# Adding expert outputs to the result in HBM: full tiles by scatters that add, one load instead of two ahead of the branch

## Chip, cores and metric

One core of one Trainium2 chip. The metric is the device time of one execution in microseconds; the time before is 964.39 us, the median of three runs (959.2 to 976.06).

## What is computed

One transformer block over 4096 tokens of width 256: a linear attention with 16 heads, then a mixture of experts with 8 experts, of which each token uses its two best. The change lies in the last step of the second half:

```python
h = _layernorm(x) * (1 + cb) + sb
gate_probs = softmax(h @ Wg + bg)              # 8 experts
_, top_idx = top_k(gate_probs, 2)
selected = gate_probs * one_hot(top_idx).sum(-2)
selected = selected / (selected.sum(-1, keepdims=True) + 1e-08)
e = gelu(einsum('bsf,efh->bseh', h, W1) + b1)  # hidden width 1024
expert_out = einsum('bseh,ehf->bsef', e, W2) + b2
x = x + gb * einsum('bsef,bse->bsf', expert_out, selected)
```

A token therefore receives two expert outputs, and each is added to its row of the result.

## The kernel before

The first half (attention) leaves the rows of x in SBUF and stores them to the result tensor `out` in HBM. Routing then computes the two experts of every token. Each token's normalised row is written twice into `routed`, a table in HBM with one region per expert, by indirect DMAs that GpSimd issues, 128 rows each (`send`). A row carries its gate weights and its token number; places of the table that no token fills carry a number outside of `out`.

The second half works through **blocks**. A block is 256 or 128 consecutive rows of one expert's region, that is two tiles or one tile of 128 rows. There are 5 early blocks of two tiles (they take only full 256-row blocks of the first 12 of the 32 token tiles), 23 further blocks of two tiles, 8 single blocks that always run, and two groups of single blocks, `once` (4) and `twice` (3), each behind a branch on `left`, a count that routing computes. In the profiled execution `once` runs and `twice` does not, so 40 blocks with 68 tiles run. After the early blocks come seven two-tile blocks, then eight times two two-tile blocks and a single one (`order_of`, lines 1231 to 1234).

For each block, `load` (line 1027) puts five DMAs on SP's queue: `w1` (1 MB), `b1`, the block's rows `xg`, `w2` (1 MB) and `b2`. `prepare` transposes the rows on TensorE, `hidden` (line 1083) makes the first matrix product and the GELU, `project` (line 1101) the second product, and VectorE scales it to tiles `y0` and `y1` of 128 x 256. `run` (line 1241) orders this: at each block it issues the loads of this block and the two that follow, does `hidden` of this block, `prepare` of the next, then `project` and `add_to_out` of the block before. Pools bound how far things run ahead: 3 buffers for `w1`, 4 for `w2`, 4 for `xg` and for each of `y0` and `y1`.

`add_to_out` (line 1122) adds a block's tiles to `out`, all of it on GpSimd's queue: for each tile a gather of its 128 rows of `out` into an SBUF tile `acc` (in profiles `hT<-out_dram,who`, since `acc` lies in an old `hT` buffer), then for each tile a GpSimd addition and a scatter back (`out_dram<-hT,who`). Rows outside of `out` are skipped. Within a block, tiles are declared independent, since a token occurs once per expert; between blocks every gather waits until the scatters of the block before have landed.

Engines issue in the order in which the program's steps are written, up to the last early block (a wrapper, line 28, adds the order; its line 36 is what profiles show for those instructions). After it only GpSimd keeps this order, and a scheduler orders the other engines. Around the early blocks, a table of steps (line 1222) puts the rest of routing between blocks: after block 1's product, the last route's first 16 sends; after block 2's, its last 8 sends and the table of the later blocks; after blocks 2 and 3, the stores of the remaining chunks of `out`.

The main blocks end at the branch (lines 1270 to 1284). Before it, `run(order_of[EARLY:], once[:2])` names two blocks of `once` as following, so that two blocks of `once` are loaded ahead of the branch and the other two inside it.

Of the kernel before, what the change touches and what calls it, by code (L numbers as in the profile page):

```python
# [15 lines left out]
ALU = mybir.AluOpType  # L16
# [8 lines left out]
BT = BLK // P  # L25
# [23 lines left out]
def adaln_block_kernel(  # L49
# [18 lines left out]
    on = SimpleNamespace(pe=nc.tensor, dve=dve, act=nc.scalar, pool=nc.gpsimd, sp=nc.sync)  # L68
# [18 lines left out]
    EARLY = 5  # L87
# [53 lines left out]
    token = const.tile([P, NCH, TPC], I32, tag="token", name="token")  # L141
# [51 lines left out]
    with tc.tile_pool(name="attn", bufs=1) as attn, tc.tile_pool(  # L193
# [24 lines left out]
        at = KB * P + E * HB  # L218
# [256 lines left out]
        with tc.tile_pool(name="ps_c", bufs=1, space=bass.MemoryType.PSUM) as ps_c:  # L475
# [83 lines left out]
            for s in range(NT + LAG):  # L559
# [6 lines left out]
                if s >= LAG:  # L566
                    add_context(s - LAG)
                    after_context(s - LAG)
                    i, rest = divmod(order[s - LAG], 3)
# [121 lines left out]
    def parked(i: int):  # L691
        return hT[i].rearrange("p kb (z d) -> p (kb z) d", d=D)
# [326 lines left out]
    w2_v = w2.rearrange("e (hb p) f -> e p hb f", p=P)  # L1019
    IN_RANGE = "the table holds rows and experts that exist"  # L1020

    accs = [parked(0)[:, BT * z : BT * (z + 1), :] for z in range(2)]

    def tiles_of(b: int):
        return BT if b < EARLY + PAIRED else 1
# [1 line left out]
    def load(b: int):  # L1027
        nt = tiles_of(b)
        first = nc.values_load(
            where[0:1, 0, b : b + 1], engines=[ENG.SP], min_val=0, max_val=E * N - nt * P,  # L1030
            skip_runtime_bounds_check_because=IN_RANGE,
        )
        e = nc.values_load(
            where[0:1, 1, b : b + 1], engines=[ENG.SP], min_val=0, max_val=E - 1,
            skip_runtime_bounds_check_because=IN_RANGE,
        )
        w1_sb = w1_pool.tile([P, KB, H], FP, tag="w1", name="w1_sb")
        on.sp.dma_start(w1_sb, w1_v[ds(e, 1)].squeeze(0))
        b1_sb = xpool.tile([P, HB], FP, tag="b1", name="b1_sb")
        on.sp.dma_start(b1_sb, b1_d[ds(e, 1)].squeeze(0))  # L1040
        xg = xpool.tile([P, BT, ROW], FP, tag="xg", name="xg")
        ins = on.sp.dma_start(
            xg[:, :nt, :], routed[ds(first, nt * P), :].rearrange("(j p) w -> p j w", p=P)
        )
        if b < EARLY:
            apart(ins, early_loads, later_sends)
        w2_sb = w2_pool.tile([P, HB, D], FP, tag="w2", name="w2_sb")
        on.sp.dma_start(w2_sb, w2_v[ds(e, 1)].squeeze(0))
        b2_sb = xpool.tile([P, D], FP, tag="b2", name="b2_sb")
        on.sp.dma_start(b2_sb, b2_d[ds(e, 1)].squeeze(0).partition_broadcast(P))  # L1050
        return xg, w1_sb, b1_sb, w2_sb, b2_sb

    def prepare(b: int, xg):

        nt = tiles_of(b)
        xT = bpool.tile([P, KB, BLK], FP, tag="xT", name="xT")
        for kb in range(KB):
            pt = ps_b.tile([P, BLK], FP, tag="b", name="ptb")
            for j in range(nt):
                on.pe.transpose(  # L1060
                    pt[:, j * P : (j + 1) * P], xg[:, j, kb * P : (kb + 1) * P], ident
                )
            on.act.activation(  # L1063
                xT[:, kb, : nt * P], pt[:, : nt * P], AF.Identity,
                bias=mod_sb[:, 2, kb : kb + 1], scale=mod_sb[:, 3, kb : kb + 1],
            )
        return xT

    def weights_of(b: int, xg):

        nt = tiles_of(b)
        who = npool.tile([P, BT], I32, tag="who", name="who")
        on.dve.tensor_copy(who[:, :nt], xg[:, :nt, D + E].bitcast(I32))  # L1073
        g = bpool.tile([P, BT, E], FP, tag="g", name="g")
        on.dve.tensor_tensor(
            g[:, :nt, :], xg[:, :nt, D : D + E],
            mine[:, b : b + 1, :].to_broadcast([P, nt, E]), ALU.mult,
        )
        gs = npool.tile([P, BT], FP, tag="gs", name="gs")
        on.dve.tensor_reduce(gs[:, :nt], g[:, :nt, :], AX.X, ALU.add)  # L1080
        return who, gs

    def hidden(b: int, xT, b1_sb, w1_sb):
        rows = tiles_of(b) * P
        gl = bpool.tile([P, HB, BLK], FP, tag="gl", name="gl")
        for hb in range(HB):
            ph = ps_a.tile([P, BLK], FP, tag="a", name="ph")
            for kb in range(KB):
                on.pe.matmul(  # L1089
                    ph[:, :rows],  # L1090
                    w1_sb[:, kb, hb * P : (hb + 1) * P],
                    xT[:, kb, :rows],
                    start=(kb == 0),
                    stop=(kb == KB - 1),
                )
            on.act.activation(  # L1096
                gl[:, hb, :rows], ph[:, :rows], AF.Gelu_apprx_tanh, bias=b1_sb[:, hb : hb + 1]
            )
        return gl

    def project(b: int, gl, w2_sb, b2_sb, who, gs):

        ys = []
        for j in range(tiles_of(b)):
            py = ps_b.tile([P, D], FP, tag="b", name="py")
            for hb in range(HB):
                on.pe.matmul(  # L1107
                    py,
                    gl[:, hb, j * P : (j + 1) * P],
                    w2_sb[:, hb, :],  # L1110
                    start=(hb == 0),
                    stop=(hb == HB - 1),
                )
            y = xpool.tile([P, D], FP, tag=f"y{j}", name="y")
            on.dve.scalar_tensor_tensor(y, py, gs[:, j : j + 1], gb_bc, ALU.mult, ALU.mult)  # L1115
            on.dve.scalar_tensor_tensor(y, b2_sb, gs[:, j : j + 1], y, ALU.mult, ALU.add)
            ys.append(y)
        return ys

    n_added = 0  # L1120

    def add_to_out(b: int, ys, who):
        nonlocal n_added
        acc = accs[n_added % len(accs)]
        n_added += 1
        rows = FIRST * TPC * P if b < EARLY else N
        done = []
        for j in range(len(ys)):
            ins = on.pool.indirect_dma_start(
                acc[:, j, :], None, out[0, :rows], IndirectOffsetOnAxis(ap=who[:, j : j + 1], axis=0),  # L1130
                bounds_check=rows - 1, oob_is_err=False,
            )
            done.append((j, ins))
        for j, y in enumerate(ys):
            on.pool.tensor_tensor(acc[:, j, :], acc[:, j, :], y, ALU.add)
            ins = on.pool.indirect_dma_start(
                out[0, :rows], IndirectOffsetOnAxis(ap=who[:, j : j + 1], axis=0), acc[:, j, :], None,
                bounds_check=rows - 1, oob_is_err=False,
            )
            for i, other in done:  # L1140
                if i != j:
                    tc.declare_no_dep(
                        ins.ins, other.ins, reason="a token is at most once among an expert's rows"
                    )
            done.append((j, ins))


    on.pe, on.dve, on.act, on.pool, on.sp = (
# [82 lines left out]
    order_of = list(range(EARLY + PAIRED - 2 * FIXED))  # L1231
# [3 lines left out]
    once = [EARLY + PAIRED + FIXED + j for j in range(ONCE)]  # L1235
# [29 lines left out]
    def flush():  # L1265
        nonlocal pending
        add_to_out(pending[0], project(*pending), pending[-2])
        pending = None

    done = set()  # L1270
# [3 lines left out]
        left[0:1, 0:1], min_val=UNITS, max_val=UNITS + ONCE + TWICE,  # L1274
        skip_runtime_bounds_check_because=IN_RANGE,
    )
    run(order_of[EARLY:], once[:2])
    flush()
    with tc.If(n_left > UNITS):  # L1279
        run(once, [])  # L1280
# [35 lines left out]
```

## Time and profile before

| | |
|---|---|
| median of 3 runs | 964.39 us |
| the profiled execution | 958.09 us |
| its span in the profile | 956.4 us |
| TensorE busy | 864.0 us, 90% of the span |
| GpSimd busy | 402.9 us, 42% |
| gathers of `out` rows, `hT<-out_dram,who` | 68, 1047 ns of GpSimd each, 4.9 us median to landing |
| scatters, `out_dram<-hT,who` | 68, 1018 ns of GpSimd each, 4.9 us median to landing |
| GpSimd additions of two 128 x 256 tiles | 68, 737 ns each |
| sends, `routed<-row,dest_i` | 64, 1048 ns of GpSimd each, 2.5 us median to landing |
| HBM read and written | 122.02 MB and 57.71 MB |

PE is TensorE, DVE VectorE, ACT ScalarE, POOL GpSimd and SP the engine whose queue issues the loads. In a timeline each line gives start, duration, engine, source line, operation, output from input, and in brackets how long the engine had been idle before and what ended that. In the table of windows each line gives the window, its length, and the busy time of each engine with its number of instructions.

### The profile page before, as it was taken

The page shows a single profiled execution, that of the slowest core. Times are in us where ns is not written, and L with a number is a line of the kernel's source. Part 1 is how long each engine was busy: PE and PEld are TensorE (multiplying, and loading weights), DVE is VectorE, ACT ScalarE, POOL GpSimd, SP SyncE. Part 2 cuts the span into 40 slices and gives each one's busy share as a digit, 9 for nine tenths or more (in the row PEclk, how much of TensorE's full clock was granted, in tenths as well). Part 3 has the DMA queues.
Part 4 walks back from the last instruction along what each step waited for, and adds up shares of the span by engine and source line. Part 5 has one row for each costly group of instructions (what it writes and reads, how often), then busy time and mean ns, then how long its engine had stood idle before and what let it go on. Part 6 is the DMA issues. An engine that isn't in the chain of part 4 may idle for free. (4 is left out here: it accounts for less than half of the span.)

```text
span 956.4 us, 12974 instructions
## 1 busy us (share of the span) xinstructions
PE 864.0 (90%) x4578; PEld 648.8 (68%) x4578; DVE 386.1 (40%) x943; ACT 347.9 (36%) x638; POOL 402.9 (42%) x377
## 2 busy tenths in 40 slices
PE   7979999999999795699779999999999999999760
PEld 4544444555545574578668888898888888888650
DVE  4454553988888747767312111111111112111110
ACT  4314442344344334455322332333333333342410
POOL 2000000588989507465744343443433433334532
PEclk9979999999999997789979999999999999999985
DMA  9999930132000013595488666677777777777510
GB/s 334 351 344 351 351 102 22 59 115 70 1 1 2 1 45 111 196 363 211 142 314 291 227 194 220 218 250 237 255 232 238 254 240 226 247 239 236 162 46 14
DMA packets 122952, 179.57 MB, mean 188 GB/s; under 512 B 12957, under 2 KB 101571, under 8 KB 122885
## 3 DMA queue, kind: packets, MB, share of 16 engines
q1 hardware_dynamic: 113040, 152.78, 49.3%
q0 software_dynamic: 9840, 25.93, 7.8%
q8 instruction: 37, 0.61, 0.3%
q14 instruction: 31, 0.25, 0.1%
q10 hardware_dynamic: 4, 0.00, 0.0%
HBM read 122.02 MB, written 57.71 MB: 188 GB/s over the span
## 5 line engine op out<-in xcount | busy, mean ns | idle before, releaser
L1096 ACT ACTIVATE gl<-ph,b_sb 128x256 f32<-128x256 f32 (+1 forms) x280 | 122.5, 438 | 273.8 <-PE ph L1089 267.4
L1107 PE MATMUL py<-w_sb,gl 128*128 128x256 f32 x960 | 214.3, 381 | 0.0
L1089 PE MATMUL ph<-xT,w_sb 128*128 128x256 f32 (+1 forms) x1120 | 207.5, 343 | 0.6 <-ACT xT L1063 0.6
L1089 PEld LDWEIGHTS ph<-xT,w_sb 128*128 128x128 f32 x1120 | 184.5, 191 | 20.4 <-ACT xT L1063 0.8
L1107 PEld LDWEIGHTS py<-w_sb,gl 128*128 128x128 f32 x960 | 180.9, 191 | 23.5
L1115 DVE SCALAR_TENSOR_TENSOR y<-py,gs,gb_bc 128x256 f32<-128x256 f32 x60 | 28.9, 482 | 269.8 <-PE py L1107 261.5
L36 POOL DMA_INDIRECT hT<-out_dram,who x68 | 71.2, 1047 | 152.6 <-DMA out_dram<-hT,who 134.6
L277 PE MATMUL pq<-wq,hT 128*128 128x512 f32 x256 | 118.3, 604 | 1.2 <-DVE qs L36 1.2
L277 PE MATMUL pk<-wk,hT 128*128 128x512 f32 x256 | 115.7, 604 | 0.3 <-ACT hT L178 0.3
L36 POOL TENSOR_TENSOR hT<-hT,y 128x256 f32<-128x256 f32 x68 | 50.1, 737 | 110.6 <-DMA hT<-out_dram,who 104.3
L36 POOL DMA_INDIRECT routed<-row,dest_i x64 | 67.1, 1048 | 61.3 <-DVE st L36 19.3
L277 PEld LDWEIGHTS pk<-wk,hT 128*128 128x128 f32 x256 | 48.1, 194 | 59.8 <-issue 54.7
L277 PEld LDWEIGHTS pq<-wq,hT 128*128 128x128 f32 x256 | 46.0, 189 | 49.5 <-issue 45.9
L36 POOL DMA_INDIRECT out_dram<-hT,who x68 | 69.2, 1018 | 19.0 <-POOL hT L36 18.2
L36 POOL TENSOR_TENSOR qs<-qs,qsum 128x1024 f32<-128x1024 f32 x30 | 58.1, 1938 | 15.6 <-DVE qsum L36 15.6
L36 DVE TENSOR_TENSOR qs<-qs,pk 128x1024 f32<-128x1024 f32 x31 | 37.8, 1221 | 62.0 <-ACT ka L438 43.8
L1073 DVE COPY who<-xg 128x2 int32<-128x2 int32 (+1 forms) x35 | 6.1, 173 | 109.4 <-DMA xg<-routed 99.4
L483 POOL MEMSET qs<- 128x8 f32 x8 | 0.9, 117 | 112.0 <-PE pt L175 80.8
L36 ACT ACTIVATE qs<-qs 128x1024 f32<-128x1024 f32 x32 | 33.8, 1055 | 38.1 <-DVE qs L36 38.1
L438 ACT ACTIVATE ka<-pk 128x1024 f32<-128x1024 f32 x24 | 24.6, 1024 | 57.2 <-PE pk L277 57.2
L36 DVE TENSOR_REDUCE qmax<-pq 128x16 f32<-128x1024 f32 x32 | 38.6, 1206 | 13.9 <-PE pq L277 13.8
L36 POOL TENSOR_TENSOR ka<-ka,nk_bc 128x1024 f32<-128x1024 f32 x18 | 42.4, 2358 | 0.0
(253 smaller groups left out, 954.8 us busy)
## 6 DMA issues: line engine op xcount, KB each, us to landing
w_sb<-in_L_ffn_W_dram SPq DMA_DIRECT2D x80, 1024.0 KB, 5.6
routed<-pad SPq DMA_DIRECT2D x32, 1088.0 KB, 13.1
x<-in_L_attn_x_dram SPq DMA_DIRECT2D x16, 512.0 KB, 6.8
xg<-routed SPq DMA_DIRECT2D x28, 272.0 KB, 5.3
b_sb<-b_d SPq DMA_DIRECT2D x40, 128.0 KB, 5.2
out_dram<-x SPq DMA_DIRECT2D x8, 512.0 KB, 5.3
xg<-routed SPq DMA_DIRECT2D x12, 136.0 KB, 5.3
ka<-in_L_wmod_dram SPq DMA_DIRECT2D x3, 512.0 KB
```

The source lines that it names most:

```text
L36: ins = getattr(self.engine, name)(*args, **kwargs)
L277: nc.tensor.matmul(pw[:, half * 512 : (half + 1) * 512], hT[i][:, kb, t * P : (t + 1) * P], w[:, kb, half * 512 : (half + 1) * 512], start ...
L438: nc.scalar.activation(k_tile(n), pk, AF.Identity)
L483: nc.gpsimd.memset(qs[:, :, (h + 1) * HW - 1 : (h + 1) * HW], 1.0)
L1073: on.dve.tensor_copy(who[:, :nt], xg[:, :nt, D + E].bitcast(I32))
L1089: on.pe.matmul(ph[:, :rows], w1_sb[:, kb, hb * P : (hb + 1) * P], xT[:, kb, :rows], start=(kb == 0), stop=(kb == KB - 1),)
L1096: on.act.activation(gl[:, hb, :rows], ph[:, :rows], AF.Gelu_apprx_tanh, bias=b1_sb[:, hb : hb + 1])
L1107: on.pe.matmul(py, gl[:, hb, j * P : (j + 1) * P], w2_sb[:, hb, :], start=(hb == 0), stop=(hb == HB - 1),)
L1115: on.dve.scalar_tensor_tensor(y, py, gs[:, j : j + 1], gb_bc, ALU.mult, ALU.mult)
```

## The change

Tiles that can't hold skipped rows are added by the DMA itself: an indirect scatter from `y` to `out` with addition as its operation, with no gather, no GpSimd addition and no `acc`. These are both tiles of the early blocks and the first tile of the 23 other two-tile blocks, 33 of the 68 that run. The last tile of every other block may be partial and is treated as before, in the order gather, scatter that adds for the full tile, addition, scatter. Each of the two `acc` buffers holds one tile instead of two. The blocks of `once` that are named as following, and so loaded ahead of the branch, are one instead of two.

```diff
@@ add_to_out
-        for j in range(len(ys)):
+        partial = None if b < EARLY else len(ys) - 1
...
+        if partial is not None:
+            acc = accs[n_added % len(accs)]
+            n_added += 1
             ins = on.pool.indirect_dma_start(
-                acc[:, j, :], None, out[0, :rows], IndirectOffsetOnAxis(ap=who[:, j : j + 1], axis=0),
-                bounds_check=rows - 1, oob_is_err=False,
+                acc, None, dest, index(partial), bounds_check=rows - 1, oob_is_err=False
             )
...
         for j, y in enumerate(ys):
-            on.pool.tensor_tensor(acc[:, j, :], acc[:, j, :], y, ALU.add)
+            if j != partial:
+                ins = on.pool.indirect_dma_start(
+                    dest, index(j), y, None, bounds_check=rows - 1, compute_op=ALU.add
+                )
+                apart_from_others(ins)
+        if partial is not None:
+            on.pool.tensor_tensor(acc, acc, ys[partial], ALU.add)
+            done.pop(0)
             ins = on.pool.indirect_dma_start(
-                out[0, :rows], IndirectOffsetOnAxis(ap=who[:, j : j + 1], axis=0), acc[:, j, :], None,
-                bounds_check=rows - 1, oob_is_err=False,
+                dest, index(partial), acc, None, bounds_check=rows - 1, oob_is_err=False
             )
...
-    run(order_of[EARLY:], once[:2])
+    run(order_of[EARLY:], once[:1])
```

`apart_from_others` declares the DMAs of one block's tiles independent, as the loop before did.

More of the change, by code (lines that the diff above doesn't have):

```diff
@@ L1020, in adaln_block_kernel @@
     IN_RANGE = "the table holds rows and experts that exist"
-    accs = [parked(0)[:, BT * z : BT * (z + 1), :] for z in range(2)]
+    accs = [parked(0)[:, z, :] for z in range(2)]
     def tiles_of(b: int):
@@ L1123, in add_to_out, with index, apart_from_others @@
         nonlocal n_added
-        acc = accs[n_added % len(accs)]
-        n_added += 1
         rows = FIRST * TPC * P if b < EARLY else N
+        dest = out[0, :rows]
+        partial = None if b < EARLY else len(ys) - 1
         done = []
-        for j in range(len(ys)):
+        def index(j):
+            return IndirectOffsetOnAxis(ap=who[:, j : j + 1], axis=0)
+        def apart_from_others(ins):
+            for other in done:
+                tc.declare_no_dep(
+                    ins.ins, other.ins, reason="a token is at most once among an expert's rows"
+                )
+            done.append(ins)
+        if partial is not None:
+            acc = accs[n_added % len(accs)]
+            n_added += 1
             ins = on.pool.indirect_dma_start(
-                acc[:, j, :], None, out[0, :rows], IndirectOffsetOnAxis(ap=who[:, j : j + 1], axis=0),
-                bounds_check=rows - 1, oob_is_err=False,
+                acc, None, dest, index(partial), bounds_check=rows - 1, oob_is_err=False
             )
-            done.append((j, ins))
+            done.append(ins)
         for j, y in enumerate(ys):
-            on.pool.tensor_tensor(acc[:, j, :], acc[:, j, :], y, ALU.add)
+            if j != partial:
+                ins = on.pool.indirect_dma_start(
+                    dest, index(j), y, None, bounds_check=rows - 1, compute_op=ALU.add
+                )
+                apart_from_others(ins)
+        if partial is not None:
+            on.pool.tensor_tensor(acc, acc, ys[partial], ALU.add)
+            done.pop(0)
             ins = on.pool.indirect_dma_start(
-                out[0, :rows], IndirectOffsetOnAxis(ap=who[:, j : j + 1], axis=0), acc[:, j, :], None,
-                bounds_check=rows - 1, oob_is_err=False,
-            )
[L1140 to L1145, printed above, removed]
+                dest, index(partial), acc, None, bounds_check=rows - 1, oob_is_err=False
+            )
+            apart_from_others(ins)
     on.pe, on.dve, on.act, on.pool, on.sp = (
```

## Prediction

> **What bounds the kernel now.** I read the chain of waits first. It names GpSimd's round trips to HBM:
>
> ```profile
> DMA 31%; POOL 8%; issue 8%; POOLq 1%
> DMA hT<-out_dram,who 19%; DMA out_dram<-hT,who 13%; POOL hT L36 5%; POOL out_dram L36 3%; POOLq L36 1%; POOLq L1273 0%; POOLq L1279 0%
> ```
>
> A chain that ends last needn't have set the pace, so the table of windows comes next:
>
> ```profile
> 560.00:600.00 40.00, 40.00 (x191) 35.20 (x191) 6.95 (x21) 12.71 (x27) 14.67 (x16) 1.00 0.68 218
> 910.00:957.00 47.00, 13.96 (x77) 12.22 (x75) 2.91 (x6) 2.95 (x8) 13.93 (x15) 0.68 0.06 19
> ```
>
> From 520 to 880 PE is busy 40.00 of every 40 us at clock 1.00. There the additions are hidden; taking them away earns nothing. Time can be won where PE is idle after routing: at 473 to 484, and from 901. The timeline of the first place, PE, then SP, then POOL:
>
> ```profile
> 465.72 7.07 PE L36 MATMUL ph<-xT,w_sb 128*128 128x256 f32 x32
> 484.26 1.09 PE L36 MATMUL ptb<-ident,xg 128*128 128x128 f32 x4 [11.48 <-DMA xg<-routed]
> ```
> ```profile
> 457.64 0.40 SPq L36 DMA_DIRECT2D w_sb<-in_L_ffn_W_dram  x1
> ...
> 481.00 0.39 SPq L36 DMA_DIRECT2D xg<-routed  x1
> ```
> ```profile
> 460.76 0.97 POOL L36 DMA_INDIRECT routed<-row,dest_i  x1 [0.31 <-issue]
> 462.04 1.06 POOL L36 DMA_INDIRECT hT<-out_dram,who  x1 [0.30 <-issue]
> ...
> 468.20 1.02 POOL L36 DMA_INDIRECT out_dram<-hT,who  x1 [0.28 <-POOL hT L36]
> 469.52 0.97 POOL L36 DMA_INDIRECT routed<-row,dest_i  x1 [0.30 <-issue]
> ```
>
> PE waits 11.48 us for the rows of the first later block; SP can't load them before the last send has landed; and the last 8 sends stand on POOL behind block 0's two gathers, additions and scatters (462.04 to 469.52). The second place, the last four blocks (`once`), PE and then SP:
>
> ```profile
> 897.88 3.73 PE L1089 MATMUL ph<-xT,w_sb 128*128 128x128 f32 x32
> 907.87 0.69 PE L1060 MATMUL ptb<-ident,xg 128*128 128x128 f32 x2 [6.25 <-DMA xg<-routed]
> 908.35 5.13 PE L1107 MATMUL py<-w_sb,gl 128*128 128x256 f32 x16
> ```
> ```profile
> 883.77 0.33 SPq L1050 DMA_DIRECT2D b_sb<-b_d  x1
> 901.65 0.38 SPq L1038 DMA_DIRECT2D w_sb<-in_L_ffn_W_dram  x1
> 902.27 0.33 SPq L1040 DMA_DIRECT2D b_sb<-b_d  x1
> 903.13 0.33 SPq L1042 DMA_DIRECT2D xg<-routed  x1
> ```
>
> SP holds the fourth block's `w1` from 884 until PE has finished the third block's hidden product (897.88 + 3.73 = 901.61). Its `xg` is queued behind; PE idles 6.25 us, and the product after it runs slower (5.13 us; the same 16 matmuls took 3.62 at 894.43). Last, POOL's end:
>
> ```profile
> 942.70 0.72 POOL L36 TENSOR_TENSOR hT<-hT,y 128x256 f32<-128x256 f32 x1 [1.65 <-DMA hT<-out_dram,who]
> 943.70 0.99 POOL L36 DMA_INDIRECT out_dram<-hT,who  x1 [0.28 <-POOL hT L36]
> ```
>
> The last `y` is ready at 925.08 (DVE 924.59 + 0.49), its addition starts 17.6 us later. POOL trails all the way: a `y` of 537.6 is added at 559.05, one of 887.3 at 915.44. So the end is POOL's backlog.
>
> **What the Trainium skill says.** Page "DMA: Bandwidth & Descriptors", section "SWDGE vs HWDGE vs iDMA": an accumulating DMA can only be issued by GpSimd; the new scatters stay on this queue. "Rules for kernel authors": the accumulate reads its destination and writes it later, so blocks still have to wait for each other; no duration is given and the trace has none. "Anatomy of one DMA": about 2.0 us plus bytes/436e3, an estimate of 2.3 us for 131072 bytes. The quiet tail agrees for plain ones (gather issue 940.02 to addition 942.70: 2.68), the loaded stage doesn't (median 4.9). "Issuing engines are not separate DMA queues": all share 16 engines, which is why loads stretch these DMAs.
>
> **Part 1, early blocks: -6.2 us.** The built order of instructions shows block 0's first scatter-add ahead of the 16 sends, its second between the 16 and the 8. The first needs `y0`, ready at 435.15, while POOL idles until 440.41: hidden, and only a `y0` later than 440.41 would push the sends back, one for one. Between 461.73 (460.76 + 0.97) and the eighth-last send then stands one issue: 461.73 + 0.30 + 1.02 + 0.30 = 463.35 instead of 469.52, so 6.17 us. I price the issue like a plain scatter (1.02); at 2 us, 5.2 remain. Last send, SP's `xg` and behind it `w2`, three stores and the next block's loads all move with it; PE idles 5.3 instead of 11.5. Next late is block 6's `xg` (VectorE gets it at 498.1, PE needs it at 500.45), and it stands on the same queue and moves too.
>
> **Part 2, the load: -8.1 us.** The early load of `once`'s second block goes behind SP's branch. SP gets there after the first block's `b2` at 859.11 and that `w1` has a wait for PE until 864.91 anyway, so 5.4 us cover a branch that now takes at most 2.2 (873.46 to 875.61). What counts is the buffers: with two `w1` tiles taken outside the branch only one of three rotates inside, hence the wait for the third block. In the changed program's waits, the fourth `w1` waits for the second block's hidden product: 894.2 (890.54 + 3.84 less overlap) instead of 901.61. `xg` follows at 895.8, lands at 900.5 with the 4.74 us of before (903.13 to 907.87), before PE's 901.6. PE gains 6.25, plus 1.5 (5.13 - 3.62) and 0.3 for the cold transposes.
>
> **Part 3, POOL's backlog: -13.9 us.** Per later two-tile block one gather (1.04 + 0.31), one addition (0.74) and one scatter (1.02) go, one scatter-add (1.02 + 0.31) comes. In series after the gather lands, 0.72 + 0.28 + 1.02 + 0.04 + 0.74 + 0.28 + 1.01 = 4.1 becomes 2.0. POOL's cycle of 14.1 (551.25 to 565.38) would be about 12 against PE's 14.25 (ptb 500.45 to 514.70); two pairs and a single, about 32 against 35.7. Over 7 pairs and 8 such triples that is some 45 us of room for a 22 us backlog. The early blocks, with no gather, should already clear most of it. POOL then waits for `y`. A scatter-add waiting for `y0` holds back only the addition and scatter of `y1`, which comes later still; the two smaller `acc` cost nothing, as a gather waits for the scatters before it anyway. With zero backlog, the tail in the old time, moved by part 2: `y` at 887.3, 899.2, 905.9, 913.3, 916.8; each single costs a landing of 2.4, a gather to addition of 2.7 and 1.0, some 6.1, more under loads; the last scatter goes at about 921.5, 4.7 after its `y` against 18.6 (943.70 - 925.08).
>
> The unknown is X, a scatter-add's issue to landing. From below 2.5 (the sends), from above 9.8 (a gather and a scatter in series, 4.9 each); below 2.5 I exclude, it also reads. I take 6. Inside these ends it is hidden: it starts with `y0`, 3.5 us before `y1`, and the other scatter lands 6 us after `y1`. VectorE's next write of `y0` waits for it, four blocks on. Moving about 33 x 128 KB less to SBUF in the PE-bound stage earns nothing.
>
> **Sum.** 6.2 + 8.1 + 13.9 = 28.2. From the last scatter to the end stay 12.7 us (956.4 - 943.70). Span 928.2; with the 1.7 around it 929.9. The median shown is 1.0066 of the profiled execution, so 936.
>
> **Rivals.** (a) *The backlog stays.* The gather of 551.25 comes 0.5 us after a `w2` load (550.74), the scatters beside a `w1` load (557.65): POOL may be held on the loads' beat, and fall back onto it. Against: the saved 2 us put the next gather at 562.5, between two loads. Then part 2 doesn't reach the end, since POOL needs no earlier `y`; part 1 and some 3 us of the last pairs remain: 947 span, 955. (b) *The load doesn't come earlier*, SP being held at the branch: 28.2 - 8.1 leaves 936.3, 944. (c) *Slower: the scatter-add is slow.* POOL's pair takes 1.36 + X; two and a single (10.5, 766.33 to 776.82) exceed PE's 35.7 from X = 11.2. Once four `y` buffers are full, PE stalls. At X = 14: first gather at 522, 7 x 15.4 + 8 x 41.2 + 3 x 6.4 gives 979 for the last, +3.7 and +12.7 an end of 995, or 1003. For it: a read and a write per row on DMA engines that are 0.64 to 0.78 busy; against: plain round trips sum to 9.8.
>
> **Chances.** All three parts 0.66, 923 to 944 alone (X and the tail's landings). (a) 0.13, (b) 0.09, (c) 0.09, else 0.03. The range 923 to 955 leaves out (c) and half the rest. 2% is about what a measurement here tells from no change: faster means below 945.1; this holds most of the first case and half of (b), so 0.70; (a) and rests 0.19; slower 0.11.
>
> **What would show it.** The eighth-last send starts near 463 and PE's wait there is near 5 us; no PE wait ahead of the fourth `once` block; POOL's additions waiting for `y` on VectorE from 600 on, and the last scatter within 6 us of the last `y`. Wrong, if scatter-adds land after more than 11 us, or if PE shows gaps between 520 and 880.

## The result, and the profile after

The changed kernel takes 957.3 us (median of 20 runs, 952.34 to 962.63), the kernel before 968.93 (20 runs beside it, 959.20 to 976.06). The ratio is 0.9889, 95% interval 0.9866 to 0.9913: 1.1% faster, where 2.9% was forecast. The profiled execution took 959.75 us with a span of 958.0. The profile of before (958.09) was quicker than any of these 20 runs of before, so the two profiles can't be subtracted; each stage has to be read by itself.

In the text blocks are counted from 0: block 5 is the first after the five early ones. The expectations on record call it "the fifth block", and what they call the third early block is block 3.

The chain of waits of the changed kernel, where the one of before had DMA and POOL at its head and no PE:

```profile
PE 81%; DVE 6%; another core or an unknown queue 4%; POOL 2%; DMA 2%; issue 2%; ACT 2%; POOLq 0%; ACTq 0%; DVEq 0%
```

POOL's round trips are gone from it. The 4% of "an unknown queue", some 38 us on a kernel that runs on one core, wasn't in the chain of before.

**From block 5 on, the forecast came true but for the tail.** The table of windows (the window, its length, the busy time of PE, PE's weight loads, DVE, ACT and POOL with their instructions, the clock, DMA share and GB/s):

```profile
560.00:600.00 40.00, 40.00 (x193) 35.23 (x192) 5.70 (x17) 13.62 (x29) 12.07 (x12) 1.00 0.69 215
910.00:957.00 47.00, 27.14 (x182) 24.89 (x180) 5.32 (x20) 12.56 (x35) 13.98 (x15) 0.85 0.21 69
```

PE is full as before, and the last 47 us hold 27 us of PE work where they held 14. The timeline of the fourth `once` block, PE and then SP:

```profile
919.84 3.73 PE L1089 MATMUL ph<-xT,w_sb 128*128 128x128 f32 x32
923.41 0.38 PE L1060 MATMUL ptb<-ident,xg 128*128 128x128 f32 x2
923.63 3.62 PE L1107 MATMUL py<-w_sb,gl 128*128 128x256 f32 x16
```
```profile
916.36 0.38 SPq L1038 DMA_DIRECT2D w_sb<-in_L_ffn_W_dram  x1
...
917.84 0.33 SPq L1042 DMA_DIRECT2D xg<-routed  x1
```

No bracket stands ahead of the transposes (6.25 us before): `w1` was issued at 916.36, ahead of the third block's product (919.84), and the next product takes 3.62 instead of 5.13. POOL's end:

```profile
944.17 1.05 POOL L36 DMA_INDIRECT hT<-out_dram,who  x1 [1.59 <-DMA out_dram<-hT,who]
947.04 0.72 POOL L36 TENSOR_TENSOR hT<-hT,y 128x256 f32<-128x256 f32 x1 [1.82 <-DMA hT<-out_dram,who]
948.03 1.00 POOL L36 DMA_INDIRECT out_dram<-hT,who  x1 [0.28 <-POOL hT L36]
```

The last `y` is ready at 938.83 (DVE 938.35 + 0.48), the last scatter goes 9.2 us later instead of 18.6, and the end comes 10.0 after it instead of 12.7.

**Ahead of block 5 something else happened.** PE, then ACT, around block 3's hidden product:

```profile
468.50 0.47 PE L36 MATMUL ph<-xT,w_sb 128*128 128x256 f32 x1 [0.37 <-issue]
483.30 2.07 PE L36 MATMUL ph<-xT,w_sb 128*128 128x256 f32 x4 [14.33 <-issue]
```
```profile
454.80 0.47 ACT L36 ACTIVATE gl<-ph,b_sb 128x256 f32<-128x256 f32 x1 [0.39 <-issue]
482.77 0.47 ACT L36 ACTIVATE gl<-ph,b_sb 128x256 f32<-128x256 f32 x1 [24.64 <-remote]
```

The product stops after 20 of its 32 matmuls, because the five buffers that take the results are full and ACT, which empties them with its GELUs, stands still for 24.64 us (without the stall it waits 5.09 us here, for PE, as e1 shows below); "remote" says only that the profile knows no releaser. ACT goes on at 482.77, and PE half a microsecond later. What POOL and SP do meanwhile:

```profile
472.73 1.61 POOL L36 DMA_INDIRECT out_dram<-y,who  x1 [0.30 <-issue]
474.64 0.99 POOL L36 DMA_INDIRECT routed<-row,dest_i  x1 [0.30 <-issue]
...
483.56 0.97 POOL L36 DMA_INDIRECT routed<-row,dest_i  x1 [0.30 <-issue]
```
```profile
470.63 0.70 SPq L36 DMA_DIRECT2D b_sb<-b_d  x1
486.01 0.39 SPq L36 DMA_DIRECT2D xg<-routed  x1
```

POOL issues the 16 sends, the scatter-add and the 8 sends without a pause. Part 1 of the forecast is there, since one issue stands between the two runs of sends where two gathers, two additions and two scatters stood. But PE no longer waits for the rows that it brings sooner: no PE wait for `xg` of block 5 is left. VectorE is held up as well: the scaling of block 1's second tile comes at 478.52, 9.57 us after the first tile's and again marked "remote", though PE's product was over at 462.33. Block 5's product starts at 515.49 instead of 493.54, 22 us later; from there to the end are 442.6 us instead of 462.8. Of the 22 us, 3.1 lie ahead of block 0, whose hidden product starts at 412.26 instead of 409.14. From there to block 5 are 103.2 us instead of 84.4.

### The profile page after: what moved, and what is told of

Same layout as the page of the kernel before. It is cut to its first block, busy times and chain, and to the rows that moved or that the text cites. A ratio compares the mean times of both kernels' runs of the same rounds, so it can differ in the third digit from the quotient of the medians.

```text
span 958.0 us, 12819 instructions
## 1 busy us (share of the span) xinstructions
PE 871.0 (91%) x4578; PEld 651.7 (68%) x4578; DVE 384.5 (40%) x943; ACT 347.0 (36%) x638; POOL 361.5 (38%) x311
## 3 DMA queue, kind: packets, MB, share of 16 engines
q0 software_dynamic: 11424, 21.61, 8.9%
## 4 chain that ended last, share of the span: by engine, by line
PE 81%; DVE 6%; another core or an unknown queue 4%; POOL 2%; DMA 2%; issue 2%; ACT 2%; POOLq 0%; ACTq 0%; DVEq 0%
PE ph L1089 21%; PE py L1107 21%; PE pk L277 12%; PE pq L277 10%; PE ph L36 3%; PE pctx L539 3%; PE py L36 2%; PE po L36 2%; PE ptb L1060 1%; DMA hT<-out_dram,who 1%; POOL qs L36 1%; PE pa L352 1%; PE pp L36 1%; PE pt L175 1%
## 5 line engine op out<-in xcount | busy, mean ns | idle before, releaser
L1089 PEld LDWEIGHTS ph<-xT,w_sb 128*128 128x128 f32 x1120 | 184.5, 191 | 20.4 <-ACT xT L1063 0.8
L36 POOL DMA_INDIRECT hT<-out_dram,who x35 | 36.7, 1050 | 141.2 <-DMA out_dram<-hT,who 120.4
L36 POOL DMA_INDIRECT out_dram<-y,who x33 | 52.4, 1589 | 96.4 <-DVE y L1116 55.7
L36 PE MATMUL ph<-xT,w_sb 128*128 128x256 f32 x160 | 42.4, 421 | 19.7 <-issue 15.8
L36 POOL TENSOR_TENSOR hT<-hT,y 128x256 f32<-128x256 f32 x35 | 25.2, 720 | 81.7 <-DVE y L1116 41.9
L36 PEld LDWEIGHTS ph<-xT,w_sb 128*128 128x128 f32 x160 | 32.9, 211 | 28.0 <-issue 17.4
L438 ACT ACTIVATE ka<-pk 128x1024 f32<-128x1024 f32 x24 | 24.6, 1024 | 57.6 <-PE pk L277 57.6
L36 DVE TENSOR_REDUCE qmax<-pq 128x16 f32<-128x1024 f32 x32 | 38.6, 1206 | 13.9 <-PE pq L277 13.8
```

The source lines that it names most:

```text
L36: ins = getattr(self.engine, name)(*args, **kwargs)
L438: nc.scalar.activation(k_tile(n), pk, AF.Identity)
L1089: on.pe.matmul(ph[:, :rows], w1_sb[:, kb, hb * P : (hb + 1) * P], xT[:, kb, :rows], start=(kb == 0), stop=(kb == KB - 1),)
```

## The experiments

Two explanations stood against each other at first: T1, a stall that comes and goes in both kernels and that the profile of before happened to miss; T2, the scatters that add lengthen the routing stage. In the table, "block 5" is the start of its first hidden product, "blocks 0-4" the time to there from the start of block 0's, "rest" the time from there to the end of the span, "scatter - y" the time from the last `y` to the last scatter, all from the profiled execution. "Before" is the median of the kernel before on the same chip; kernels with the same median there ran together. Each such set ran on another chip, and no chip was used twice.

| label | kernel | median us | before | ratio, 95% interval | block 5 | blocks 0-4 | rest | scatter - y |
|---|---|---|---|---|---|---|---|---|
| e1 | changed | 933.69 | 955.43 | 0.9777 (0.9746 to 0.9808) | 490.0 | 80.4 | 442.3 | 9.0 |
| e2 | before | 954.28 | 955.43 | 0.9979 (0.9958 to 0.9999) | 494.1 | 84.8 | 463.7 | 19.7 |
| e3 | scatters only | 937.67 | 955.43 | 0.9822 (0.9791 to 0.9854) | 488.2 | 80.4 | 445.6 | 3.9 |
| e4 | load only | 955.65 | 955.43 | 0.9994 (0.9970 to 1.0018) | 499.1 | 84.7 | 455.5 | 18.9 |
| e5 | changed | 952.30 | 962.67 | 0.9870 (0.9823 to 0.9917) | 508.8 | 97.6 | 442.2 | 8.9 |
| e6 | before | 963.90 | 962.67 | 0.9996 (0.9976 to 1.0017) | 509.4 | 93.2 | 462.7 | 18.7 |
| e7 | early blocks the old way | 947.09 | 962.67 | 0.9820 (0.9769 to 0.9872) | 503.7 | 91.3 | 442.2 | 8.7 |
| e8 | later blocks the old way | 959.14 | 962.67 | 0.9958 (0.9939 to 0.9977) | 510.5 | 96.5 | 451.0 | 15.4 |
| e9 | changed | 954.39 | 964.14 | 0.9909 (0.9882 to 0.9937) | 514.3 | 98.4 | 442.3 | 8.9 |
| e10 | changed, one pause of 6 us | 945.40 | 964.14 | 0.9832 (0.9788 to 0.9876) | 501.5 | 89.9 | 444.1 | 9.0 |
| e11 | changed, 12 pauses | 947.90 | 964.14 | 0.9842 (0.9801 to 0.9882) | 504.7 | 92.2 | 442.5 | 9.2 |
| e12 | early blocks the old way | 948.30 | 964.14 | 0.9858 (0.9816 to 0.9899) | 501.3 | 89.5 | 444.1 | 9.2 |
| e13 | changed | 934.52 | 956.92 | 0.9782 (0.9749 to 0.9816) | 490.5 | 80.3 | 442.3 | 9.0 |
| e14 | changed, 12 short pauses | 935.76 | 956.92 | 0.9789 (0.9761 to 0.9818) | 491.4 | 81.5 | 442.9 | 9.0 |
| e15 | changed, pauses in two routes | 939.43 | 956.92 | 0.9832 (0.9800 to 0.9864) | 496.4 | 86.9 | 441.9 | 8.9 |
| e16 | before, pauses in two routes | 964.66 | 956.92 | 1.0085 (1.0051 to 1.0118) | 505.6 | 91.6 | 461.6 | 18.2 |
| e17 | as e14 | 946.09 | 962.86 | 0.9817 (0.9780 to 0.9855) | 499.5 | 88.3 | 442.9 | 9.2 |
| e18 | as e15 | 945.05 | 962.86 | 0.9805 (0.9766 to 0.9843) | 502.3 | 88.0 | 442.3 | 9.3 |

### Both kernels once more, and each half of the change alone (e1 to e4)

e1 and e2 are the kernels unchanged. e3 keeps the scatters and puts the load back; e4 is the kernel before with only the load moved:

```diff
 e3, in the changed kernel
-    run(order_of[EARLY:], once[:1])
+    run(order_of[EARLY:], once[:2])
 e4, in the kernel before
-    run(order_of[EARLY:], once[:2])
+    run(order_of[EARLY:], once[:1])
```

> The changed kernel once more, for a second profile. Theory T1 (the profile of before that the forecast was built on was a quick execution, and a stall of about 10 us in the routing stage comes and goes in both kernels): ratio to before 0.985 to 0.992, and the fifth block's first hidden product starts somewhere from 493 to 516 us, not at the same place as in the first profile. Theory T2 (the change itself lengthens the routing stage by 10 to 20 us): the fifth block starts within 3 us of 515.5 again.

> The kernel before once more, for a second profile. T1: the profiled span is 962 to 972 us, near the median of its runs, and the fifth block's first hidden product starts 5 to 15 us later than the 493.5 of the first profile. T2: the span is 955 to 960 us plus noise and the fifth block starts within 3 us of 493.5. Ratio 1.00 under both.

> Only the scatters that add; the load in front of the branch stays as before. My forecast's steps: 8.1 us longer than the changed kernel, ratio about 0.997 when the changed kernel stands at 0.989. T1: the same. T2: the routing stage is as in the changed kernel (fifth block at about 515), ratio 0.995 to 0.999. If the load is hidden anyway: ratio 0.989, as the changed kernel.

> Only the load is moved; additions by gather and scatter as before. The PE wait of 8 us ahead of the fourth single of the once list is gone, but the queue of additions on POOL is still full at the end. If POOL's backlog sets the end, ratio 0.998 to 1.000. If PE sets it: ratio 0.991 to 0.993. T2: routing stage as in before (fifth block near 493.5).

The same changed kernel took 933.69 us here, 2.2% less than before. That it is close to the forecast of 936 is in part luck: the kernel before is at 955.43 here, not at 964.39, and the gain is 21.7 us where 28.4 was forecast. Both theories had expected less gain. Its PE and ACT at the same places:

```profile
467.98 7.07 PE L36 MATMUL ph<-xT,w_sb 128*128 128x256 f32 x32
480.02 1.09 PE L36 MATMUL ptb<-ident,xg 128*128 128x128 f32 x4 [4.96 <-DMA xg<-routed]
```
```profile
454.80 0.47 ACT L36 ACTIVATE gl<-ph,b_sb 128x256 f32<-128x256 f32 x1 [5.09 <-PE ph L36]
455.66 0.47 ACT L36 ACTIVATE gl<-ph,b_sb 128x256 f32<-128x256 f32 x1 [0.39 <-PE ph L36]
```

ACT waits for nothing but PE, block 3's GELUs come at PE's pace of 0.86 us, and PE's wait for the rows of block 5 is 4.96 where 5.3 was forecast (11.48 before, 10.37 in e2). The span is 25.7 us shorter than in the first profile of the changed kernel, 25.5 of it ahead of block 5 and 22.9 of that in blocks 0 to 4. So T2 as a property of the program falls: this program has no long stall of its own. On this chip neither kernel shows one, and e2's block 5 starts where the first profile of before had it.

The load alone is worth nothing in time (0.9994), as expected for a full queue on POOL that sets the end. But the profiles don't bear this reason out: from block 5 to the end e4 takes 8.2 us less than e2, though its last scatter still trails its `y` by 18.9. Blocks 0 to 4 are alike. The profiled execution of e4 is 5.1 us late already at block 0 (414.40 against 409.31), ahead of anything that the edit moves; where its other executions lose the gain isn't shown.

Put on top of the scatters the load is worth 4.0 us (937.67 - 933.69), half of the forecast's 8.1. PE does gain the 8: from block 5 to the end of PE's last product are 422.2 us in e1 and 430.6 in e3. But with the `y` of the last blocks spread by PE's wait, e3's last scatter follows its `y` after 3.9 us, in e1 after 9.0.

### On another chip, and the change split by blocks (e5 to e8)

e5 and e6 are again the unchanged kernels. e7 and e8 keep both ways of adding (`add_by_gathers` is the kernel before's function):

```diff
+    def add_to_out(b: int, ys, who):
 e7
+        (add_by_gathers if b < EARLY else add_by_scatters)(b, ys, who)
 e8
+        (add_by_scatters if b < EARLY else add_by_gathers)(b, ys, who)
```

> The changed kernel a third time. Its first profile reached the fifth block's first hidden product at 515.5 us, its second at 490.0, and each ends as much later or earlier (958.0 and 932.3 us). Theory C (the routing stage of the same program is stretched by a stall of PE, ACT and DVE together on some chips, not on others): the fifth block starts near 490 and the ratio to before is 0.975 to 0.980, or it starts after 505 and the ratio is 0.985 to 0.992. Theory R (the stall is random from execution to execution): executions of both sorts in one set of runs, spread over 20 us.

> The kernel before a third time, beside it on the same chip. Theory C: if the changed kernel stalls, this one does too, its wait of PE for the rows of the fifth block (11.5 and 10.4 us in two profiles) is shorter than 5 us or gone, its span is 965 to 972 us; if not, 955 to 958 us and the wait is 10 to 12 us. Ratio 1.00.

> Scatters that add from the sixth block on, but the five early blocks by gather, addition and scatter. My forecast's part 1 is given back: PE waits 10 to 12 us for the rows of the fifth block instead of 5.0, the rest as in the changed kernel. 6 us longer than the changed kernel: ratio 0.983 to 0.986 where the changed kernel has 0.978. If the early blocks' scatters that add are what lengthens the routing stage (theory T2): as quick as the changed kernel or quicker.

> Scatters that add for the five early blocks only, gather, addition and scatter from the sixth on; the load is early. PE gains the 6 us of part 1 and the 8 us of part 2, but POOL's queue is again full at the end. Forecast's view (POOL sets the end by a cycle of 14.1 us for each pair): PE's last product comes 12 to 15 us earlier than in before, the last scatter only 0 to 9 us earlier, ratio 0.990 to 1.000. If PE sets the end: 0.985 or less.

Here ACT stands still in all four profiles ("remote" ahead of GELUs: 24.1, 21.8, 20.4 and 23.7 us), at the same two places: in block 1 and at the start of block 3. All runs of e5 lie within 5 us of each other, so it isn't chance from execution to execution: theory C. (No chip was met twice, so the runs don't tell the chip from the hour.) The kernel before has the stall too, and no PE wait for block 5's rows is left in e6: the stall has taken its place. As e6's profiled execution took 973.86, 10 us above its median, this rests on e7, whose early blocks are those of the kernel before: PE has no such wait there either, and 0.9 us in e12 below.

The surprise is e7: with the early blocks done by gather, addition and scatter it is 5.2 us quicker than the changed kernel, where 6 us slower was expected. On this chip the early scatters cost what they should gain. The ratio of e8, 0.9958, lies where a POOL that sets the end would put it, but its profile doesn't fit that: from block 5 on the last `y` comes 8.0 us earlier than in e6 and the last scatter 11.3, where 0 to 9 in all was expected. What keeps e8 slow lies in blocks 0 to 4, 96.5 us against 91.3 in e7.

### Is it POOL's unbroken row of issues? (e9 to e12)

In e5 and in the first profile ACT stands still while POOL issues indirect DMAs one behind the other. In the kernel before, and in e7, block 0's gathers and additions interrupt that row between the 16 and the 8 sends. Theory H: the change took away the pause in which ACT caught up. e10 puts a pause there, e11 many short ones; neither uses the results:

```diff
 e10, in send, ahead of its loop
+            if which == (2,):
+                for _ in range(8):
+                    row = self.row[2][:, 0, :D]
+                    on.pool.tensor_tensor(parked(0)[:, 3, :], row, row, ALU.add)
 e11, behind each send
+                    if len(self.chunks) == 3 and k == 1:
+                        row = self.row[t // TPC][:, t % TPC, :D]
+                        on.pool.tensor_tensor(parked(0)[:, 3, :], row, row, ALU.add)
```

> The changed kernel a fourth time, as the reference for the next three. Two cases so far. Smooth (as in its second profile): ACT passes the five early blocks without long waits, PE waits 5.0 us for the rows of the fifth block, ratio 0.978. Stalled (as in its first and third profile): ACT stands idle 15 to 35 us in all ahead of its GELU instructions while POOL issues the last route's sends one behind the other, ratio 0.987 to 0.989.

> The changed kernel, with eight additions of 128x256 on POOL (about 0.75 us each, 6 us in all, result unused) between its last 16 and its last 8 sends, where the kernel before has the gathers and additions of block 0. Theory H (on some chips ACT hardly gets on while POOL issues indirect DMAs back to back, and the change took away the pause between the two runs of sends in which ACT caught up): where the reference is stalled, ACT's idle time ahead of GELUs shrinks by 4 us or more, and the kernel is as quick as the reference or quicker (0 to -5 us) in spite of 6 us more on POOL; where it is smooth, 6 us slower. Rival (the stall has nothing to do with POOL's issues): ACT's idle time stays as in the reference, and the kernel is 0 to 6 us slower in both cases.

> The changed kernel, with one addition of 128x256 on POOL (0.75 us, result unused) after every second of the last route's 24 sends, 12 in all. Theory H: where the reference is stalled, ACT's idle time ahead of GELUs falls below 12 us, the sends end about 10 us later, and the fifth block starts no later than in the reference. Where it is smooth: 7 to 10 us slower, since PE already waits for the last sends. Rival: idle time as in the reference, and where that is stalled the fifth block starts up to 10 us later.

> The early blocks by gather, addition and scatter, the later full tiles by scatters that add. Where the reference is stalled: 5 us quicker than it, as in the run before. Where it is smooth: 5 to 6 us slower than it (ratio about 0.984), PE waiting 10 to 12 us for the rows of the fifth block, as my forecast's part 1 has it.

A chip with the stall again. Six microseconds of useless work on POOL make the kernel 9.0 us quicker (945.40 against 954.39), 12 additions spread among the sends 6.5 us, and e12 repeats e7 (6.1 us quicker). Blocks 0 to 4 take 89.9, 92.2 and 89.5 us instead of 98.4. POOL and ACT of e10:

```profile
471.15 1.61 POOL L36 DMA_INDIRECT out_dram<-y,who  x1 [0.31 <-issue]
472.19 6.06 POOL L36 TENSOR_TENSOR hT<-row 128x256 f32<-128x256 f32 x8
```
```profile
472.36 0.47 ACT L36 ACTIVATE gl<-ph,b_sb 128x256 f32<-128x256 f32 x1 [15.84 <-remote]
473.77 1.93 ACT L36 ACTIVATE gl<-ph,b_sb 128x256 f32<-128x256 f32 x5 [0.94 <-remote]
```

ACT's 15.8 us of standing still are not ended by the pause: they are as long in e9, and in both kernels they end while POOL is at the scatter-add ahead of the place of the pause, 1.2 us after its start in e10 and 1.1 in e9. What differs is what follows. In e10 ACT has caught up before the additions are over: five GELUs in 1.93 us. In e9, without the pause, the GELUs come singly through the 8 sends:

```profile
475.82 1.61 POOL L36 DMA_INDIRECT out_dram<-y,who  x1 [0.30 <-issue]
```
```profile
476.94 0.47 ACT L36 ACTIVATE gl<-ph,b_sb 128x256 f32<-128x256 f32 x1 [15.78 <-remote]
...
491.13 0.47 ACT L36 ACTIVATE gl<-ph,b_sb 128x256 f32<-128x256 f32 x1 [3.05 <-remote]
```

The idle time marked "remote" fell by only 3.7 us (22.4 to 18.7), just short of the 4 expected, and the time by more than the 0 to 5 expected.

In e11 block 3 has no such wait at all. The lists of ACT's waits from 420 to 500 us (us in total, times, longest), e9 and then e11:

```profile
ACT gl L36 <- remote: 22.4, 5, 15.8
```
```profile
ACT gl L36 <- remote: 1.7, 1, 1.7
```

The rival, a stall that has nothing to do with POOL, expected idle times as in e9. It falls. Nor do these GELUs depend on the sends: in e1 they pass from 454.80 on, in the midst of the 16 sends (441.04 to 462.36). VectorE recovers with ACT: ahead of the `y` of the early blocks it has 19.4 us of "remote" in e9, 2.1 in e12, none in e17 and e18 below. What is left in e11 is in block 1, beside the sends of the route before, where e11 has no pauses.

### How long, and where (e13 to e18)

e14 and e17 shorten e11's additions to 128x64; e15 and e18 put the 128x256 ones behind every second send of the last two routes (`self.chunks[0] >= FIRST` for the condition); e16 does that to the kernel before:

```diff
 e14 and e17, against e11
-                        row = self.row[t // TPC][:, t % TPC, :D]
-                        on.pool.tensor_tensor(parked(0)[:, 3, :], row, row, ALU.add)
+                        row = self.row[t // TPC][:, t % TPC, :64]
+                        on.pool.tensor_tensor(parked(0)[:, 3, :64], row, row, ALU.add)
 e15, e16 and e18, against e11
-                    if len(self.chunks) == 3 and k == 1:
+                    if self.chunks[0] >= FIRST and k == 1:
```

> The changed kernel, reference for the next three. Stalled (ACT idle over 15 us ahead of GELUs of the third early block while POOL issues sends): ratio 0.987 to 0.991. Smooth: 0.978.

> The changed kernel with short pauses: an addition of 128x64 on POOL (some 0.3 us, result unused) after every second of the last route's 24 sends. Theory H, if any pause will do: ACT's idle time falls as with the longer pauses (below 5 us in the place of 15.8), PE waits less than the 10.6 us for the rows of the fifth block, and the kernel is 3 to 6 us quicker than with the longer ones, ratio 0.977 to 0.981 where the reference is stalled. If the pause must be long enough for ACT to get through: in between the reference and the longer pauses, 0.984 to 0.989. Smooth: 2 to 4 us slower than the reference.

> The changed kernel with an addition of 128x256 on POOL after every second send of the last two routes (16 and 24 sends; results unused). Theory H: the earlier and smaller stall, in the second early block (about 8 us of ACT idle), goes too. POOL has a gap of over 5 us behind the first 16 sends, so these pauses cost nothing there. 3 to 8 us quicker than pauses in the last route alone (0.984): ratio 0.976 to 0.981 where the reference is stalled. Smooth: 7 to 10 us slower than the reference.

> The kernel before with the same pauses in the last two routes. Theory H: its stall goes as well, but PE waits longer for the rows of the fifth block (11 us without stall, plus some 10 us of pauses): ratio 0.99 to 1.01. If the stall is what hid the rest of the forecast's gain, this kernel minus the one with pauses in two routes is what was forecast, 24 to 30 us (2.5 to 3.1% of before). If the gain is lost elsewhere too, no more than 15 us.

> Short pauses (additions of 128x64 on POOL after every second of the last route's 24 sends) once more, for a chip on which the kernel before takes 962 us or more, as the three on which the changed kernel stalled. Theory H, any pause will do: ACT's idle time ahead of GELUs of the third early block, 15.8 us in the changed kernel there, falls below 5 us; ratio 0.978 to 0.982 against the changed kernel's 0.987 to 0.991 there. If short pauses don't let ACT through: 0.986 to 0.991. Where before takes 955 to 957 us: 0.979, as in the run before.

> Pauses of 128x256 in the last two routes once more. Where before takes 962 us or more, theory H: the idle time of ACT ahead of GELUs of the second early block (about 8 us) goes as well, ratio 0.974 to 0.980, quicker than pauses in the last route alone had there (0.984). If that stall has another cause: 0.983 to 0.986. Where before takes 955 to 957 us: 0.983.

e13 to e16 met a chip without the stall, so for the stall they say only what pauses cost where none is needed: 1.2 us for short ones and 4.9 for pauses in two routes (2 to 4 and 7 to 10 were expected), 7.7 in the kernel before. With pauses alike in both the change is worth 25.2 us (964.66 - 939.43), without 22.4, too near to be told apart.

e17 and e18 met a chip where the kernel before takes 962.86 us; the changed kernel itself wasn't run on it, and the 5.0 us that remain in e17 are the sign that it has the stall. Short pauses are enough: block 3 has no unexplained wait in e17, 5.0 us in block 1 remain, and the ratio is 0.9817 where the changed kernel itself had 0.9870 to 0.9909 in its three sets of runs with the stall. In e18 no such wait is left in either block: the smaller stall in block 1 has the same cause. In time it brought 1.0 us more, not to be told from nothing (0.9805, where 0.974 to 0.980 was expected).

e15 and e18 are one kernel on two chips, 5.6 us apart, which is about what the kernel before differs by (956.92 to 962.86). In their profiles most of it lies ahead of block 0 (409.46 and 414.24); blocks 0 to 4 take 86.9 and 88.0 us, so with these pauses the stall is nearly gone. The changed kernel itself differs by more than before does: against the means without the stall (934.1 changed, 956.2 before) it takes 23.2, 18.2 and 20.3 us longer in its three sets with the stall, the kernel before 12.7, 6.5 and 8.0. So the change is worth some 22 us without the stall and 10 to 12 with it. The profiles agree: with the stall, blocks 0 to 4 take 17 to 23 us longer in the changed kernel (97.6 to 103.2 against 80.4), and 5 to 7 us longer where the early blocks are added as before (89.5 in e12 and 91.3 in e7 against 84.4 to 84.8). That the stall accounts for the whole excess is argued; e7 and e10 to e12 got 5 to 9 us of it back.

## Why the prediction was wrong

**The step that failed is to take blocks 0 to 4 as the profile of before shows them: in part 1, "PE idles 5.3 instead of 11.5", and in the sum, "The median shown is 1.0066 of the profiled execution, so 936."** From block 0's first hidden product to block 5's that profile has 84.4 us, and part 1 makes it 78.2. The changed kernel's recorded profile has 103.2: ACT stands still there while POOL issues, and PE comes later than the rows, with no wait left to shorten. For all that a usual execution has more than the profiled one, the last factor adds 6.3 us, as if every stage were longer by 0.66%. They aren't: from block 5 to the end every profile of the kernel before has 462.7 to 463.7 us, and every profile of the changed kernel 442.2 to 442.6. What differs lies ahead of block 5, in blocks 0 to 4 and, by up to 8.5 us over all profiles, ahead of them. The profile of before showed blocks 0 to 4 without the stall, the recorded profile of the changed kernel has it, and with it part 1 has the wrong sign.

**Part 1, -6.2 us.** Without the stall the mechanism is right and the size short. PE's wait went from 11.5 and 10.4 to 5.0 and 4.9, and blocks 0 to 4 from 84.4 and 84.8 to 80.4 and 80.3 us (two profiles each), 4.2 less. One term mis-sized is the issue of a scatter-add: 1.59 us on average (33 of them in 52.4 us) instead of the 1.02 of a plain scatter. Another is the product behind the wait, which takes 9.3 us instead of 8.6 and 8.3 and which the forecast left as it was. With the stall the step is wrong as put: "PE idles 5.3 instead of 11.5" needs a PE that gets to the wait, and PE came later than the rows. With the early blocks of the kernel before, 10 to 11 us of the stall are hidden in that wait (none of it is left in e7, 0.9 us in e12), and ACT can catch up during POOL's gathers and additions between the sends; the changed kernel has taken both away. Early scatters then cost 5 to 6 us (e5 against e7, e9 against e12).

**Part 2, -8.1 us.** Right on PE (422.2 against 430.2 us from block 5 to the end of the last product, e1 and e2), 4.0 us in time. What a part is worth hangs on the order: from block 5 to the end the load takes away 8.2 us when it comes first (e2 to e4) and 3.3 when it comes last (e3 to e1), the scatters 13.2 or 18.1. The first order comes near the forecast's 8.1 and 13.9.

**Part 3, -13.9 us.** Right: POOL waits for `y` (in e1, 27 of the scatter-adds and additions of the later blocks do, for 55.2 us in all). Measured are -10.7 (19.7 to 9.0, e2 and e1) for the last scatter and, not forecast, -2.7 from it to the end (12.7 to 10.0). With the 8.0 of part 2 these are the 21.4 us by which the rest shrank, against 22.0 forecast.

The term that fails is the tail: "the last scatter goes at about 921.5, 4.7 after its `y`". It goes 9.0 after it. The `y` of the last four singles do come about as forecast, 7.2, 7.0 and 3.5 us apart (6.7, 7.4 and 3.5 in the forecast; moved by its own 8.1 us, the last three would stand at 906.5, 913.5 and 917.0 rather than 905.9, 913.3 and 916.8, on which nothing hangs). What doesn't hold is "With zero backlog", and the "some 6.1" of a single. In e1 the first of the four has its `y` at 895.61, and POOL issues its gather after that:

```profile
897.08 1.06 POOL L36 DMA_INDIRECT hT<-out_dram,who  x1 [5.40 <-DVE g L1075]
```

Its addition (901.46) comes 5.9 us after its `y`. From gather to gather are then 8.1, 6.8 and 6.5 us, since each waits for the scatter before it. So POOL stays 5 us behind, none of the four additions waits for `y`, and the last short step makes the 5 us 8.0. What held the first gather isn't settled: the profile names a VectorE instruction of the fourth block, and the scatter ahead of it, begun at 890.66, moved its rows beside that block's loads.

**The unknown X**, taken as 6 us between 2.5 and 9.8: a scatter-add lands 3.7 to 8.4 us after its issue, median 5.3, in e1 (3.9 in e3 and e13). Rival (c) never came near, and neither did (a) or (b): the load came early and the backlog went, but for the 5 us of the tail. None of the rivals was the one that came true, a stage longer than in the profile. Where that stage is as profiled, the gain was 21.7 and 22.4 us (e1, e13) against the 28.4 forecast, and 11.6 in the recorded runs.

**The signs named** show this split: the eighth-last send started at 464.6 and PE waited 5.0 us in e1, as forecast, while the recorded profile has 474.64 and no wait. The wait ahead of the fourth `once` block is gone in both. "Within 6 us of the last `y`" failed at 9. Neither sign of being wrong showed: no scatter-add took 11 us, and PE is full from 520 to 880.

**What stays open.** That ACT gets on when POOL's row of issues has pauses is shown by e10, e11, e17 and e18. How the row holds it back isn't: a pause spaces out the issues and also the row writes that they start, and no run parts the two. ACT's steps in the stall are spaced by multiples of about 0.71 us (1.43, 2.13, 2.83, 3.52 between GELUs), and SP slows too: between the issues of a block's `w1` and `b1` lie 2.2, 2.0 and 2.1 us in the stall (the first profile, e5, e9) and 0.7 in e1. Nor is it shown what differs between the chips. Another difference comes before all this: over the 20 profiles block 0's first product starts at 407.8 to 416.3 us, in both kernels and with and without the stall. It wasn't followed.

As far as these runs go, the version to take is e14/e17: 1.2 us over the changed kernel where there is no stall, and 0.9817 against 0.987 to 0.991 where there is, though measured on another chip than those.

## What to carry to other kernels

When the profiled execution is quicker than the median of the runs, find the stage in which the others lose the time before summing anything on the profile: the changed kernel may be the one that can no longer hide it. A wait that a change shortens is also slack for everything that runs beside it, and a pause in one engine's queue may be when another gets its work done; before closing either, ask what used it. And where several short blocks end a kernel, work out the tail with the lag that it starts from: each round trip that waits for the one before carries it on.

## What the runs showed of the hardware

- In three sets of runs ACT, VectorE and SP hardly advance while GpSimd issues indirect DMAs back to back (0.97 us each, 0.30 apart); in two other sets, on other chips, they do, with the same program. ACT's wait for the first GELU of block 3 is 15.8 to 24.6 us in the changed kernel against 5.1. Additions of 128x64 on GpSimd after every second issue are enough to let ACT through (e17: no such wait in block 3).
- An indirect scatter with addition costs GpSimd 1.59 us for 128 rows of 1 KB (1.02 for a plain one), and moves packets of 1024 bytes where plain ones have 4096: 11424 packets and 21.6 MB on that queue, instead of 9840 and 25.9 MB. It lands in 3.7 to 8.4 us, median 5.3 (e1).
- With scatter-adds in the later blocks the end comes 9.7 to 10.2 us after the last scatter, without them 12.2 to 12.7, though that last scatter is a plain one in both. No run here tells why.
